# Spectral convolution on Trainium2: folded blocks of x, shifted copies from SBUF to SBUF, and 64x32 tiles in the last inverse step

## The chip, the cores and the metric

The kernel runs on one core of one Trainium2 chip. The core has a matrix engine (TensorE: PE for the matmuls, PEld for the weight loads), a vector engine (DVE), a scalar engine (ACT), a general engine (GpSimd, here POOL) and SyncE (SP), which issues most of the DMAs. The engines run side by side, each through its own instructions in order, and wait for each other through semaphores. Matmuls write to PSUM; the other engines copy the results to SBUF ("evict" them). The metric is the device time of one execution in microseconds (us).

## The reference

The input is four images of 512x512 pixels with 16 channels, in float32. Two layers follow each other, each with a group norm and a residual. The first is a convolution over the whole image with a filter that is given as a quotient of polynomials; it is done in the frequency domain:

```
H = rfft2(irfft2(rfft2(b)/rfft2(a)), s=(1024, 1024));  H_full = h0 + H[0]
X = rfft2(gn(x), s=(1024, 1024))
Y = einsum('...hwi,ijhw->...hwj', X, H_full)
y = irfft2(Y)[..., :512, :512, :];  x = x + y
```

The second layer is a 3x3 convolution that is normalized by the norms of patch and kernel and passed through an arccos.

## The kernel before

The kernel has five stages. The first evaluates the filter (and takes the statistics of the group norm beside it). `forward_phase` (L617 to L699) transforms x along the image's width with matmuls, after normalization. `conv_phase` (L705 to L966) does all that belongs to one frequency of the width: transform along the height, product with the filter, and inverse along the height. A further stage does the inverse along the width, and the last one the second layer. Only the second and third stage are spoken of below.

`forward_phase` goes over 16 blocks (4 images, 4 blocks of 128 lines). A block is loaded with four DMAs and folded about the middle of the width (additions on DVE, L652; subtractions on POOL, L654), transposed on PE (L661), and multiplied by the transform's matrix (L683). Products are evicted in turn by DVE (L691) and ACT (L693) and stored.

`conv_phase` works through 513 rows, one per frequency of the width (that of 0 in two parts). Of one row:
- `load_x` and `load_g` fetch x and the filter's line. `turn_x` (L773, L775) multiplies the small transform `dfs` by a phase that belongs to the row.
- `x_part` (L786) is the transform over 64 positions along the height into 128 frequencies f, with 4 matmuls into two PSUM tiles `px`; the evictions write slot 0 of `xe`, a tile of 128 partitions with 8 slots of 128x8 values.
- The other slots hold copies of slot 0 that are shifted by 16 partitions per slot. What would be shifted beyond the end comes from a late copy `xl` with another phase: `x_late` forms it on POOL with four products (L807) into a tile `xu`, one product over all (L808) and an addition (L809). Slot 4 is written by ACT, half from slot 0 and half from `xl` (`half_shift`, L818). The other six go through DRAM: POOL stores slot 0 and `xl` (L800), and SP loads them again, shifted, a row later (`load_xe`, L824).
- `g_part` (L838) transforms the filter's line in four groups, into a ring of three PSUM tiles `pg`, evicted into `gh`.
- `mix` (L854) is the product over channels: for each frequency one matmul with `gh` as weights, in four column quarters of 32. Four groups of 64 instructions; each is evicted into `yf`.
- `over_q` (L875 to L893) transposes `yf` into `pz`, and ACT (`zq`, L882), DVE (L883 to L887) and, at the end of the row, POOL (L891, L893) form sums and differences `z` and `zd`.
- `over_g` (L912) is the last inverse step with 8 matmuls of 128x64, into one PSUM tile `py`; the eviction goes into `yo`, and POOL stores it (L923).

`px`, `pz` and `py` share one ring of three PSUM tiles (`h_psf`, tag "full"). `evict` (L736, L738) gives two of three evictions to ACT and the third to DVE. `step(n)` interleaves five rows: `mix` of row n with `g_part` of n+1, `over_q` of n-1, `x_part`, `x_late` and `half_shift` of n+2, `turn_x` of n+3 and `over_g` of n-2, in four quarters k. The order on each engine isn't exactly that of the source; it is put in order when the program is built.

Of the kernel before, what the change touches and what calls it, by code (L numbers as in the profile page):

```python
# [48 lines left out]
B = 4  # L49
# [20 lines left out]
def constants():  # L70
# [80 lines left out]
    f, sb = np.arange(F), np.arange(S)  # L151
    d = np.zeros((2, S, F, 2))
    co, si = turn(np.outer(sb + 31.5, f), F)
    d[0, :, :, 0], d[0, :, :, 1] = co, -si
    d[1, :, :, 0], d[1, :, :, 1] = si, co
    c["dfs"] = np.stack([d, np.stack([d[..., 1], -d[..., 0]], -1)], 2).reshape(P, -1)
# [5 lines left out]
    ig = np.zeros((32, 2, 2, 4, 2, 2, 2, 16))  # L162
    for s0 in range(4):
        for cx in range(2):
            for c2 in range(2):
                n = gg[:, None] * s0 + 4 * gg[:, None] * s1[None, :] + 32 * (cx + c2)
                co, si = turn(n, F)
                for b2 in range(2):
                    ig[:, cx, b2, s0, c2, 0, b2, :] = co / F
                    ig[:, cx, b2, s0, c2, 1, b2, :] = si / F  # L170
# [446 lines left out]
def forward_phase(tc, cst, x, mvs, x_d):  # L617
    nc = tc.nc
    with ExitStack() as ctx:
        cp = ctx.enter_context(tc.tile_pool(name="x_const", bufs=1))  # L620
        xp = ctx.enter_context(tc.tile_pool(name="x_in", bufs=8))
        sm = ctx.enter_context(tc.tile_pool(name="x_small", bufs=B))
        up = ctx.enter_context(tc.tile_pool(name="x_u", bufs=4))
        tp = ctx.enter_context(tc.tile_pool(name="x_t", bufs=2))
# [12 lines left out]

        for b in range(B):
            scale, bias = norm[b]
            twice = sm.tile([P, 8], F32, name="twice")  # L640
            nc.vector.tensor_add(twice, bias, bias)
            for ht in range(4):
                xt = []
                for w in range(4):
                    t = xp.tile([P, P, C], F32, name="xt")
                    nc.sync.dma_start(out=t, in_=x[b, ht * P : (ht + 1) * P, w * P : (w + 1) * P, :])
                    xt.append(t)

                su = []
                for w in range(2):  # L650
                    u = up.tile([P, P, C], F32, name="xu")
                    nc.vector.tensor_add(u, xt[w], xt[3 - w][:, ::-1, :])  # L652
                    su.append(u)
                    nc.gpsimd.tensor_sub(xt[w], xt[w], xt[3 - w][:, ::-1, :])  # L654
                halves = su + xt[:2]
                xw = tp.tile([P, 4, C, P], F32, name="xw")
                for i4 in range(4):
                    for w in range(4):
                        pt = ps_x.tile([P, 4, P], F32, name="pt")
                        for i in range(4):  # L660
                            nc.tensor.transpose(pt[:, i], halves[w][:, :, 4 * i4 + i], ident)  # L661
                        for i2 in range(2):
                            g = 2 * i4 + i2
                            dst = xw[:, w, 2 * g : 2 * g + 2, :]
                            src = pt[:, 2 * i2 : 2 * i2 + 2, :]
                            if i2 == 0 and w < 2:
                                nc.scalar.activation(dst, src, AF.Identity,
                                                     scale=scale[:, g : g + 1], bias=twice[:, g : g + 1])
                            elif i2 == 0:
                                nc.scalar.activation(dst, src, AF.Identity, scale=scale[:, g : g + 1])  # L670
                            elif w < 2:
                                nc.vector.tensor_scalar(dst, src, scale[:, g : g + 1],
                                                        twice[:, g : g + 1], ALU.mult, ALU.add)
                            else:
                                nc.vector.tensor_scalar(dst, src, scale[:, g : g + 1], None, ALU.mult)
                for rc in range(4):
                    o = op.tile([P, 2, 16, 8, C], F32, name="xo")
                    for c in range(2):
                        col = (2 * rc + c) * P
                        for i4 in range(4):  # L680
                            pf = ps_f.tile([P, 4, 16, 8], F32, name="pf")
                            for w in range(2):
                                nc.tensor.matmul(  # L683
                                    pf.rearrange("p i s t -> p (i s t)"), fwd[:, w, col : col + P],
                                    xw[:, 2 * c + w, 4 * i4 : 4 * i4 + 4, :].rearrange("p i h -> p (i h)"),
                                    start=(w == 0), stop=(w == 1),
                                )
                            dst = o[:, c, :, :, 4 * i4 : 4 * i4 + 4]
                            src = pf.rearrange("p i s t -> p s t i")[:, :, ::-1, :]
                            if c == 0:  # L690
                                nc.vector.tensor_copy(dst, src)  # L691
                            else:
                                nc.scalar.copy(dst, src)  # L693
                    for c in range(2):
                        nc.sync.dma_start(
                            out=dram(x_d[rc], None, c * X_ROW // 2 + (16 * ht * B + b) * C * 8,
                                     [B * C * 8, 16], [1, C * 8]),
                            in_=o[:, c].rearrange("p s t i -> p s (t i)"),
                        )  # L699
# [5 lines left out]
def conv_phase(tc, cst, g_d, x_d, y_d):  # L705
    nc = tc.nc
    with ExitStack() as ctx:
# [11 lines left out]
        dfs = load_const(nc, cp, cst, "dfs").rearrange("p (v n) -> p v n", v=2)  # L719
        dg = load_const(nc, cp, cst, "dg")  # L720
        ident = load_const(nc, cp, cst, "ident")
        ig = load_const(nc, cp, cst, "ig").rearrange("p (s c n) -> p s c n", s=4, c=2)
        late = load_const(nc, cp, cst, "late").rearrange("p (v f) -> p v f", v=3)

        xf_d = [tc.dram_tile([16 * C, XF], F32, name=f"xf_d{n}") for n in range(4)]
# [26 lines left out]
        def load_x(n):  # L752
# [3 lines left out]
            if plane is None:  # L756
                nc.sync.dma_start(out=t, in_=dram(x_d[rc], r, 0, [w, P], [1, w]))
            else:
                nc.gpsimd.memset(t[S:], 0.0)
                nc.sync.dma_start(out=t[:S], in_=dram(x_d[rc], r, plane * S * w, [w, S], [1, w]))  # L760
            state["x", n] = x

        def turn_x(n):
# [8 lines left out]
            t = xlp.tile([P, 2 * F], F32, name="turn")  # L772
            nc.scalar.activation(t, dfs[:, 1], AF.Identity, scale=own[:, 1, at])  # L773
            m = xlp.tile([P, 2 * F], F32, name="dfs_n", bufs=2)
            nc.vector.scalar_tensor_tensor(m, dfs[:, 0], own[:, 0, at], t, ALU.mult, ALU.add)  # L775
            state["dfs", n] = m

        def x_part(n, b):

            if b == 0:  # L780

                state["xe", n] = xep.tile([P, 8, F, 2, 2, 2], F32, name="xe")
            if b % 2 == 0:
                state["px"] = ps_f.tile([P, 2, F, 2], F32, name="px", tag="full")
# [661 lines left out]
```

## Time and profile before

| what | us |
|---|---|
| median of three runs (lowest, highest) | 18,372.5 (18,348.46, 18,387.49) |
| the profiled execution | 18,378.82 |
| its span | 18,377.0 |
| filter and statistics, 0 to 5,320 | 5,320 |
| forward, 5,320 to 6,415 | 1,095 |
| conv, 6,415 to 15,535 | 9,120 |
| inverse along the width, 15,535 to 16,610 | 1,075 |
| second layer, 16,610 to 18,377 | 1,767 |

Over the whole span PE is busy 88%, PEld 63%, DVE 61%, ACT 52% and POOL 57%. A busy share is an average over stages, so the conv stage is looked at by itself, and within it single rows. In the profile "PEclk" is the clock that PE was granted (1.00 is full speed), and "idle before, releaser" is the time in which an instruction's engine stood still ahead of it, with the instruction whose end released it.

### The profile page before, as it was taken

The numbers are of one execution on the slowest core, as the hardware profiler recorded it, in microseconds if no ns is written. First come the engines' busy times: TensorE is split into PE (matmuls) and PEld (weight loads), VectorE is DVE, ScalarE is ACT, GpSimd is POOL, SyncE is SP. The second block draws the span as 40 slices with busy tenths as digits, with TensorE's granted clock in tenths as the row PEclk, the third lists the DMA queues.
The fourth block names the chain that finished last, engine by engine and source line by source line (L and its number), as shares of the span: only waits on it lengthen the run. The fifth ranks groups of instructions, "written<-read, shape, count | busy, mean of one in ns | idle before, by whom it ended". The sixth has DMA issues, their size and how long they took to land. (4 is left out here: it accounts for less than half of the span.)

```text
span 18377.0 us, 546088 instructions
## 1 busy us (share of the span) xinstructions
PE 16100.0 (88%) x233100; PEld 11615.5 (63%) x233100; DVE 11247.9 (61%) x23131; ACT 9599.6 (52%) x19919; POOL 10502.4 (57%) x10653
## 2 busy tenths in 40 slices
PE   7788888888889988888888888888888988988888
PEld 4444444444444467777777777777767776877777
DVE  8877777777833355555555555555555554246887
ACT  4556555555632255555555555555555554106788
POOL 5566666666621166666666666666666664026776
PEclk6888988888999999999999999999999999998999
DMA  4655555555676588888888888888888887795431
GB/s 123 201 162 165 162 165 162 164 163 161 167 221 184 167 319 320 318 321 324 316 321 318 319 325 323 325 325 323 323 323 314 325 320 289 257 324 192 160 129 69
DMA packets 2918877, 4543.47 MB, mean 247 GB/s; under 512 B 117634, under 2 KB 2086492, under 8 KB 2809694
## 3 DMA queue, kind: packets, MB, share of 16 engines
q1 hardware_dynamic: 2686254, 3768.39, 60.7%
q0 software_dynamic: 174896, 605.89, 8.7%
q10 hardware_dynamic: 55296, 134.24, 2.2%
q8 instruction: 1835, 30.06, 0.6%
q14 instruction: 596, 4.88, 0.1%
HBM read 3030.71 MB, written 1477.31 MB: 245 GB/s over the span
## 5 line engine op out<-in xcount | busy, mean ns | idle before, releaser
L838 PE MATMUL pg<-c_dg,g 64*128 64x128 f32 x32832 | 2836.9, 291 | 326.6 <-ACT gh L738 163.0
L854 PE MATMUL pm<-xe,gh 128*32 128x64 f32 x131328 | 2397.8, 222 | 587.8 <-issue 354.6
L854 PEld LDWEIGHTS pm<-xe,gh 128*32 128x32 f32 x131328 | 2011.9, 110 | 1165.3 <-issue 972.6
L838 PEld LDWEIGHTS pg<-c_dg,g 64*128 64x128 f32 x32832 | 2283.3, 190 | 670.4 <-issue 253.4
L456 PE MATMUL pt<-ev_in,c_todd 128*128 128x512 f32 x4096 | 2191.1, 681 | 350.4 <-ACT ot L461 323.9
L883 DVE TENSOR_TENSOR z<-zq,pz 128x256 f32<-128x256 f32 x2052 | 861.4, 420 | 2608.4 <-ACT zq L882 2531.1
L736 DVE COPY gh<-pg 128x512 f32<-128x512 f32 x2046 | 1410.1, 689 | 1312.1 <-PE pg L838 1308.2
L379 POOL TENSOR_TENSOR x<-ab,ab 128x512 f32<-128x512 f32 x1024 | 1561.1, 1524 | 1081.7 <-ACT ab L362 1029.0
L807 POOL TENSOR_TENSOR xu<-xe,c_late 128x256 f32<-128x256 f32 x2052 | 1389.5, 702 | 860.2 <-ACT xe L738 834.6
L377 DVE RECIPROCAL dn<-dn 128x256 f32<-128x256 f32 x1024 | 1781.8, 1740 | 0.0
L456 PEld LDWEIGHTS pt<-ev_in,c_todd 128*128 128x128 f32 x4096 | 792.4, 210 | 1483.1 <-issue 640.1
L738 ACT COPY yf<-pm 128x512 f32<-128x512 f32 x2046 | 1210.9, 592 | 924.0 <-PE pm L854 909.2
L362 ACT COPY ab<-pab 128x512 f32<-128x512 f32 x2048 | 1127.9, 617 | 858.7 <-PE pab L353 609.1
L818 ACT COPY xe<-xl 64x1024 f32<-64x1024 f32 x513 | 538.5, 1050 | 1872.5 <-POOL xl L809 1872.5
L738 ACT COPY gh<-pg 128x512 f32<-128x512 f32 x2058 | 1200.0, 583 | 398.4 <-PE pg L838 389.5
L875 PE MATMUL pz<-c_ident,yf 128*128 128x128 f32 x8208 | 1377.4, 291 | 30.3 <-issue 28.5
L404 PE MATMUL pg<-c_dinv,sp 64*128 64x128 f32 x16384 | 1192.7, 301 | 117.8 <-ACT sp L393 117.8
L404 PEld LDWEIGHTS pg<-c_dinv,sp 64*128 64x128 f32 x16384 | 1084.7, 209 | 313.2 <-PE pab L353 134.1
L376 DVE TENSOR_TENSOR m<-ab,ab 128x512 f32<-128x512 f32 x1024 | 1271.4, 1242 | 0.0
L809 POOL TENSOR_TENSOR xl<-xl,xu 128x1024 f32<-128x1024 f32 x513 | 1208.9, 2357 | 40.2
L383 POOL TENSOR_TENSOR m<-m 128x256 f32<-128x256 f32 x1024 | 747.0, 730 | 746.4 <-DVE m L376 746.2
L1289 PE MATMUL pc<-l_band,xn 128*128 128x160 f32 (+2 forms) x6144 | 1072.9, 333 | 53.7 <-DVE e_o L1344 53.5
(204 smaller groups left out, 31381.8 us busy)
## 6 DMA issues: line engine op xcount, KB each, us to landing
xe<-xf_d SPq DMA_DIRECT2D x1026, 1536.0 KB, 8.4
g<-g_d SPq DMA_DIRECT2D x511, 1024.0 KB, 9.8
g_d<-st SPq DMA_DIRECT2D x64, 4096.0 KB, 31.3
ev_in<-g_d SPq DMA_DIRECT2D x1024, 256.0 KB, 4.6
g_d<-ot SPq DMA_DIRECT2D x1024, 256.0 KB, 2.5
xf_d<-xe POOLq DMA_DIRECT2D x513, 448.0 KB, 8.3
xf_d<-xl POOLq DMA_DIRECT2D x513, 448.0 KB, 5.2
x_d<-xo SPq DMA_DIRECT2D x128, 1024.0 KB, 5.1
```

The source lines that it names most:

```text
L376: nc.vector.tensor_mul(w["m"], b, a)
L377: nc.vector.reciprocal(w["dn"], w["dn"])
L379: nc.gpsimd.tensor_mul(w["x"], b, a[:, :, ::-1])
L404: nc.tensor.matmul(pg[u][:, n, k].rearrange("p a x -> p (a x)"), w["sp"][q, k, c, :], dinv[q, 2 * kp + k, c, :], start=(c == 0), stop=(c = ...
L456: nc.tensor.matmul(pt, todd[:, c, kc, hh * P : hh * P + P], ev[:, kc, c], start=(kc == 0), stop=(kc == 1),)
L736: nc.vector.tensor_copy(dst, src)
L738: nc.scalar.copy(dst, src)
L807: nc.gpsimd.tensor_mul(u[:, :, h, c], xe[:, :, h, 1 - c], bc(late[:, 1 + c], 2, [P, F, 2]))
L809: nc.gpsimd.tensor_add(xl.rearrange("p f h c k -> p (f h c k)"), xl.rearrange("p f h c k -> p (f h c k)"), u.rearrange("p f h c k -> p (f ...
L838: nc.tensor.matmul(pg[c][:, j % 4], g[half, j], dg[half], start=True, stop=True)
L854: nc.tensor.matmul(pm[32 * q : 32 * q + 32, g % 8], gh[:, f].rearrange("p c j -> p (c j)"), xe[:, :, f].rearrange("p t h c k -> p t (h c k ...
L875: nc.tensor.transpose(pz[:, t % 4].rearrange("p v q x -> p (v q x)"), y[:, at].rearrange("p g x -> p (g x)"), ident)
```

## The change

In the forward stage the blocks of 128 lines are folded about the middle of the image: block ht and block 3-ht are transformed together, ACT copies the product of the one, and DVE adds and subtracts that of the other, mirrored. So the two halves that are stored are the even and the odd part along the height.

In the conv stage `x_part` then transforms 32 positions for each parity, with 64 rows of contraction and one PSUM tile per part (real, imaginary). The phase that belongs to the row moves from the input's transform to the output's: `turn_ig` replaces `turn_x`. `over_g` works in tiles of 64x32 into two PSUM tiles. The shifted copies no longer go through DRAM: `shift` copies from slot 0 and `xl` to the other slots within SBUF, with twelve DMAs that SP issues. The intermediate product `u` has no tile of its own but is written into slot 4 of `xe`, and `xl` has two buffers. `x_part` stands ahead of `over_q` in the step. The inverse stage and the constants follow the new layout of y.

```diff
--- before
+++ after
-        xp = ctx.enter_context(tc.tile_pool(name="x_in", bufs=8))
+        xp = ctx.enter_context(tc.tile_pool(name="x_in", bufs=6))
-        up = ctx.enter_context(tc.tile_pool(name="x_u", bufs=4))
-        tp = ctx.enter_context(tc.tile_pool(name="x_t", bufs=2))
+        up = ctx.enter_context(tc.tile_pool(name="x_u", bufs=3))
+        tp = ctx.enter_context(tc.tile_pool(name="x_t", bufs=5))
+        ap = ctx.enter_context(tc.tile_pool(name="x_a", bufs=4))
...
+        def folded(b, ht):
+
...
+            return su, xt[:2]
+
+        def turned(halves, scale, bias):
+
+            xw = tp.tile([P, 2, C, P], F32, name="xw")
...
+            return xw
+
+        def transform(xw, c, rc, i4):
...
+            return pf.rearrange("p i s t -> p s t i")[:, :, ::-1, :]
+
         for b in range(B):
-            for ht in range(4):
...
+            for ht in range(2):
+                near, far = folded(b, ht), folded(b, 3 - ht)
+                for c in range(2):
+                    both = [turned(h[c], scale, (twice, None)[c]) for h in (near, far)]
+                    for rc in range(4):
+
+                        sums = [op.tile([P, 16, 8, C], F32, name=f"xo{k}") for k in range(2)]
                         for i4 in range(4):
...
+                            pa, pb = (transform(xw, c, rc, i4) for xw in both)
+                            pb = pb[:, ::-1]
+                            a = ap.tile([P, 16, 8, 4], F32, name="xa")
+                            nc.scalar.copy(a, pa)
+                            i = slice(4 * i4, 4 * i4 + 4)
+                            nc.vector.tensor_add(sums[0][:, :, :, i], a, pb)
+                            nc.vector.tensor_sub(sums[1][:, :, :, i], a, pb)
+                        for k in range(2):
+                            part = ((0, 3), (2, 1))[c][k]
+                            nc.sync.dma_start(
+                                out=dram(x_d[rc], None, part * X_ROW // 4 + (16 * ht * B + b) * C * 8,
+                                         [B * C * 8, 16], [1, C * 8]),
+                                in_=sums[k].rearrange("p s t i -> p s (t i)"),
+                            )
...
-        xf_d = [tc.dram_tile([16 * C, XF], F32, name=f"xf_d{n}") for n in range(4)]
...
-        def turn_x(n):
+        def turn_ig(n):
...
             own, at = state["own", n // 64], slice(n % 64, n % 64 + 1)
-            t = xlp.tile([P, 2 * F], F32, name="turn")
-            nc.scalar.activation(t, dfs[:, 1], AF.Identity, scale=own[:, 1, at])
-            m = xlp.tile([P, 2 * F], F32, name="dfs_n", bufs=2)
-            nc.vector.scalar_tensor_tensor(m, dfs[:, 0], own[:, 0, at], t, ALU.mult, ALU.add)
-            state["dfs", n] = m
-
-        def x_part(n, b):
-
...
+            t = xlp.tile([P, 256], F32, name="turn")
+            nc.scalar.activation(t, ig[:, 1], AF.Identity, scale=own[:, 1, at])
+            m = xlp.tile([P, 4, 2, 32], F32, name="ig_n", bufs=2)
+            nc.vector.scalar_tensor_tensor(m.rearrange("p s c n -> p (s c n)"), ig[:, 0], own[:, 0, at], t,
+                                           ALU.mult, ALU.add)
+            state["ig", n] = m
+
+        def x_part(n):
+
+            state["xe", n] = xep.tile([P, 8, F, B, 2], F32, name="xe")
+            px = [ps_f.tile([P, B, F], F32, name=f"px{c}", tag="full") for c in range(2)]
+            for b in range(B):
+                for c in range(2):
+                    half = slice(64 * c, 64 * c + 64)
+                    nc.tensor.matmul(px[c][:, b], state["x", n][half, b], dfs[half], start=True, stop=True)
+            for c in range(2):
+                evict(state["xe", n][:, 0, :, :, c], px[c].rearrange("p b f -> p f b"))
+            del state["x", n]
 
         def x_late(n):
 
             xe = state["xe", n][:, 0]
...
+            fl = xe.rearrange("p f b c -> p f (b c)")
+
+            xl = xlp.tile([P, F, B, 2], F32, name="xl", bufs=2)
+            u = state["xe", n][:, 4]
             for c in range(2):
...
+                nc.gpsimd.tensor_mul(u[:, :, :, c], xe[:, :, :, 1 - c], bc(late[:, 1 + c], 2, [P, F, B]))
+            nc.gpsimd.tensor_mul(xl.rearrange("p f b c -> p f (b c)"), fl, bc(late[:, 0], 2, [P, F, 2 * B]))
+            nc.gpsimd.tensor_add(xl.rearrange("p f b c -> p (f b c)"),
+                                 xl.rearrange("p f b c -> p (f b c)"),
+                                 u.rearrange("p f b c -> p (f b c)"))
             state["xl"] = xl
 
         def half_shift(n, half):
 
             dst, src = ((slice(0, 64), state["xe", n][64:, 0]), (slice(64, P), state["xl"][:64]))[half]
-            nc.scalar.copy(state["xe", n][dst, 4].rearrange("p f h c k -> p (f h c k)"),
-                           src.rearrange("p f h c k -> p (f h c k)"))
-
-        def load_xe(n):
-            src = xf_d[n % 4]
-            for t in (1, 5):
-                nc.sync.dma_start(
-                    out=state["xe", n][:, t : t + 3].rearrange("p t f h c k -> p t (f h c k)"),
-                    in_=bass.AP(tensor=src.tensor, offset=src.offset + t * C * XF,
-                                ap=[[XF, P], [C * XF, 3], [1, XF]]),
-                )
+            nc.scalar.copy(state["xe", n][dst, 4].rearrange("p f b c -> p (f b c)"),
+                           src.rearrange("p f b c -> p (f b c)"))
+
+        def shift(n, half):
+
+            xe, src = state["xe", n], state["xl"] if half else state["xe", n][:, 0]
+            for t in (1, 2, 3, 5, 6, 7):
+                at = C * t
+                to, of = ((slice(0, P - at), slice(at, P)), (slice(P - at, P), slice(0, at)))[half]
+                nc.sync.dma_start(out=xe[to, t].rearrange("p f b c -> p (f b c)"),
+                                  in_=src[of].rearrange("p f b c -> p (f b c)"))
 
         def g_part(n, j):
 
...
             if g % 8 == 7:
-                evict(state["y", n][:, :, g - 7 : g + 1].rearrange("p t g x -> p g t x"),
-                      pm.rearrange("p g t (h x) -> p g (t h) x", h=2))
+                evict(state["y", n][:, :, g - 7 : g + 1].rearrange("p m g c -> p g m c"), pm)
...
             if k == 0:
-                state["py"] = ps_f.tile([P, 2, 2, 8, C], F32, name="py", tag="full")
-            z, d, py = state["z", n], state["zd", n], state["py"]
-            odd, c2 = k // 2, k % 2
-            for half in range(2):
-                s0 = 2 * half + odd
...
+                state["py"] = [ps_f.tile([P, 2, 8, C], F32, name=f"py{h}", tag="full") for h in range(2)]
+            z, d, m = state["z", n], state["zd", n], state["ig", n]
+            c2 = k
+            for s0 in range(4):
+                at = (s0 + 1) % 4
+                if at % 2 == 0:
+                    zs = z[:, :, at + c2]
...
-                nc.tensor.matmul(
-                    py[64 * half : 64 * half + 64, odd], ig[:, s0, c2],
-                    zs.rearrange("p (t h) j -> p h t j", h=2),
-                    start=(c2 == 0), stop=(c2 == 1),
-                )
-            if k < 3:
+                for half in range(2):
+                    q = slice(64 * half, 64 * half + 64)
+                    nc.tensor.matmul(
+                        state["py"][half][32 * s0 : 32 * s0 + 32], m[q, s0, c2],
+                        zs[q].rearrange("p (t h) j -> p h t j", h=2), start=(c2 == 0), stop=(c2 == 1),
+                    )
+            if k == 0:
                 return
...
+            del state["z", n], state["zd", n], state["ig", n]
+            yo = yop.tile([P, 2, 2 * P], F32, name="yo")
+            for half in range(2):
+                evict(yo[:, half].rearrange("p (h j t) -> p h j t", h=2, j=C),
+                      state["py"][half].rearrange("p h t j -> p h j t"))
+            w = 2 * P
             if plane is None:
-                nc.gpsimd.dma_start(out=dram(y_d[rc], r, 0, [4 * P, P], [1, 4 * P]), in_=yo)
+                nc.gpsimd.dma_start(out=dram(y_d[rc], r, 0, [w, P], [P * w, 2], [1, w]), in_=yo)
...
-            if row(1):
-                load_xe(n + 1)
...
                 if row(1):
                     for j in range(4):
                         g_part(n + 1, 4 * k + j)
+                if row(2) and k == 0:
+                    x_part(n + 2)
                 if row(-1):
                     for t in range(4):
                         over_q(n - 1, 4 * k + t)
                 if row(2) and k == 0:
-                    for m in range(B):
-                        x_part(n + 2, m)
+                    shift(n + 2, 0)
                     x_late(n + 2)
+                    shift(n + 2, 1)
                 if row(2) and k >= 2:
                     half_shift(n + 2, k - 2)
-                if row(3) and k == 2:
-                    turn_x(n + 3)
+                if row(-1) and k == 2:
+                    turn_ig(n - 1)
                 if row(-2) and k == 2:
-                    for m in range(4):
+                    for m in range(2):
                         over_g(n - 2, m)
```

More of the change, by code (lines that the diff above doesn't have):

```diff
@@ L161, in constants @@
     gg, s1 = np.arange(32), np.arange(16)
-    ig = np.zeros((32, 2, 2, 4, 2, 2, 2, 16))
+    ig = np.zeros((2, 32, 2, 2, 4, 2, 2, 16))
     for s0 in range(4):
@@ new lines, in transform @@
+        def transform(xw, c, rc, i4):
+            col = (2 * rc + c) * P
+            pf = ps_f.tile([P, 4, 16, 8], F32, name="pf")
+            for w in range(2):
+                nc.tensor.matmul(
+                    pf.rearrange("p i s t -> p (i s t)"), fwd[:, w, col : col + P],
+                    xw[:, w, 4 * i4 : 4 * i4 + 4, :].rearrange("p i h -> p (i h)"),
+                    start=(w == 0), stop=(w == 1),
+                )
+            return pf.rearrange("p i s t -> p s t i")[:, :, ::-1, :]
```

175 lines of the change are left out of this document (60 added, 115 removed).

## Prediction

> **What bounds the kernel now.** Three views were read in this order: the table by stretches, the list of waits inside the conv stretch, and the timeline of one row by engine. Columns of the first: stretch, length, busy time of PE, PEld, DVE, ACT and POOL (instructions), granted PE clock, DMA share, GB/s.
>
> ```profile
> 5320.00:6415.00 1095.00, 1032.81 (x3074) 515.48 (x3074) 402.38 (x551) 279.71 (x513) 152.58 (x36) 0.97 0.60 182
> 6415.00:15535.00 9120.00, 8121.43 (x184680) 6487.67 (x184680) 4934.76 (x13342) 4784.71 (x8721) 5777.09 (x5653) 0.98 0.86 320
> 12009.83:12026.92 17.09, 15.71 (x361) 12.51 (x361) 9.79 (x27) 9.24 (x17) 11.27 (x11) 1.00 0.89 335
> ```
>
> The first line is the forward stretch, the second the conv stretch, the third one of its rows. Conv takes 9,120 us for 513 rows, 17.78 us each; a quiet row takes 17.09 with PE at work for 15.71. No engine is full, so a loop through several engines sets the pace. The waits of the conv stretch (waiter and line, releaser and line: total us, how often, longest) name its members:
>
> ```profile
> DVE z L883 <- ACT zq L882: 2531.1, 1579, 6.7
> ACT xe L818 <- POOL xl L809: 1872.5, 513, 6.5
> POOL xu L807 <- ACT xe L738: 834.6, 507, 7.1
> PE pm L854 <- DMA xe<-xf_d: 96.4, 70, 3.2
> ```
>
> ACT stands still 3.65 us in every row for POOL's last addition; a DMA holds PE in 70 cases for 96 us in all. The transfers that the change removes are hidden already. The timeline of that row, POOL, then ACT, then PE (start, busy time, instructions, idle before and releaser):
>
> ```profile
> 12014.17 1.36 POOL L807 TENSOR_TENSOR xu<-xe,c_late 128x256 f32<-128x256 f32 x2 [1.40 <-ACT xe L738]
> 12015.65 0.57 POOL L800 DMA_DIRECT2D xf_d<-xe  x1
> 12016.25 1.35 POOL L807 TENSOR_TENSOR xu<-xe,c_late 128x256 f32<-128x256 f32 x2
> 12017.54 1.98 POOL L808 TENSOR_TENSOR xl<-xe,c_late 128x1024 f32<-128x1024 f32 x1
> 12019.60 2.36 POOL L809 TENSOR_TENSOR xl<-xl,xu 128x1024 f32<-128x1024 f32 x1
> ```
>
> ```profile
> 12021.99 1.05 ACT L818 COPY xe<-xl 64x1024 f32<-64x1024 f32 x1 [3.73 <-POOL xl L809]
> 12023.07 0.58 ACT L738 COPY yf<-pm 128x512 f32<-128x512 f32 x1
> 12023.55 0.59 ACT L738 COPY gh<-pg 128x512 f32<-128x512 f32 x1
> 12024.02 0.39 ACT L882 COPY zq<-pz 128x256 f32<-128x256 f32 x1
> ```
>
> ```profile
> 12024.19 1.16 PE L838 MATMUL pg<-c_dg,g 64*128 64x128 f32 x14 [0.33 <-ACT gh L738]
> 12026.92 0.77 PE L854 MATMUL pm<-xe,gh 128*32 128x64 f32 x40 [0.57 <-ACT zq L882]
> ```
>
> Read as a loop: POOL starts the late copy at 12014.17 and ends the addition at 12021.96, 7.79 us. ACT then makes the shift it had waited for and works off what stood behind it, so the next row's mix starts at 12026.92, 4.96 us after the addition. Mix, g_part, transposes, x_part and the eviction lead to POOL's next start at 12031.26, 4.34 us later. 7.79 + 4.96 + 4.34 = 17.09, the length of the row.
>
> **The change, part by part.**
>
> *Forward.* The transform's matmul instructions (2,048; the page has two for each matmul, and so do all counts below) and the DMAs stay the same in number. Evictions of the products go from 256 copies on DVE and 256 on ACT to 256 copies on ACT and 512 additions or subtractions on DVE. At 0.69 us each (the DVE eviction of 128x512) DVE goes from 402 to some 580 us, beside PE's 1,033. The smaller buffer pools (6 input blocks, 3 folded) make the fold of the next pair wait for the transposes. Bounds: 0, if PE still covers it, to +107 us, eight pairs whose four additions on DVE (3.32 us each) all lie bare. I take +40, not far from the middle, as nothing in the trace places it.
>
> *Conv, removed in every row.* From POOL two DMA issues (0.57 and 0.58) and four multiplications of 0.70; from the queues 0.9 MB of stores and 3.1 MB of loads, hidden; from PE sixteen py instructions of 128x64 (1.96 us in the row) and eight px of 256 columns (1.89); turn_x, whose place an equal turn_ig takes.
>
> *Conv, added in every row.* On PE sixteen x_part instructions in g_part's form (16 take 1.16) and thirty-two of py in 64x32 tiles: by the mix (64 in 1.10) at least 0.55, by the old py at most 1.96; I take 1.0, near the mix, since four quarters work beside each other in both. PE's work falls from 15.7 to 15.7 - 1.96 - 1.89 + 1.16 + 1.0 = 14.0 us. On POOL two multiplications of 128x512 for the four of half that size: 1.27 (the sum L893) to 1.52 each (L379), against 4 x 0.70 = 2.80; I take 1.35, so the late copy takes 2.7 + 1.98 + 2.36 = 7.0 us with the gaps (bounds 6.8 and 7.4). On SP twelve SBUF copies for two loads: 3.0 MB in 64 to 448 KB. The trace has no such copy; by the old xe load (3 MB inside 8.4 us with others beside it) they take about 8 us of the engines. Lower bound 4 us, half of that; upper bound 16, twice. The whole DMA load falls from 0.86 x 17.78 = 15.3 to some 12.5 us per row and stays covered by a row's slack, for a shift of row n+2 is first read by a mix one row later.
>
> *The wait that is moved.* The multiplied copy u no longer has a tile of its own; it is written into slot 4 of xe, the slot that half_shift(n, 0) then overwrites. So half_shift(0) has to wait for POOL's addition, where before only half_shift(1) did. On ACT's queue half_shift(0) stands ahead of the second block's gh eviction and its zq (in the built program it carries the wait on POOL). In the row above those, gh at 12017.41 and zq at 12017.88, were done before ACT's wait began. Now gh(1) and zq(1) wait for the addition too. Who waits for these: PE's g_part of the third block (a pg buffer), and, since px and py now take eight tiles a row in a ring of three instead of seven, py, whose second tile takes over pz(1)'s place: it needs zq(1) and the DVE chain behind it.
>
> From the end of the addition: half_shift 1.05, gh 0.58, zq 0.38, DVE's five operations 0.42 + 0.29 + 0.29 + 0.30 + 0.28 = 1.58, together 3.6; then py 1.0, the last mix 1.1, its g_part 1.16, the eviction 0.6: 7.5 us to the next row's mix. In the row kinds where both half_shifts stand ahead it is up to 1.5 more (1.05 for the second, 0.5 for a second gh on ACT). The built order repeats six kinds of row, half of them of either sort; the mean is 8.3. Before it was 4.96.
>
> From that mix to POOL's start: mix 1.1, g_part 1.16, x_part 1.16, eviction 0.6, 4.0; in some kinds x_part stands ahead of g_part. I take 3.9 (before 4.34).
>
> Sum: 7.0 + 8.3 + 3.9 = 19.2 us at full clock, against 17.09. PE works 14.0 of it, so it stands idle 5.2 us, in one stretch while POOL ends its addition.
>
> *The clock.* What such a stretch costs, the trace of before shows (first line a gap, second line what follows; same columns as above):
>
> ```profile
> 9000.00:9001.60 1.60, 0.04 (x1) 0.03 (x1) 1.44 (x5) 0.36 (x1) 0.70 (x1) 1.00 0.78 310
> 9001.90:9005.30 3.40, 3.40 (x74) 3.00 (x62) 0.43 (x2) 0.58 (x1) 1.54 (x2) 0.50 0.53 164
> ```
>
> The granted clock changes in steps of 3.41 us. All 91 drops to 0.50 in the conv stretch followed a step in which PE was busy 0.57 or less; it came back after a step busy 0.92 or more. An idle stretch of 5.2 us always leaves one step under 0.3, so every row drops. At half clock the mix takes 1.7 to 1.9 us for 1.10 and g_part 1.9 to 2.1 for 1.16. The half clock falls on py, the last mix and g_part, all in the loop: 3.3 us of matmuls that grow by 0.5 (clock back at once) to 2.5 us (half clock throughout). I take 2.1, since the drop lasts at least one whole step.
>
> The Trainium skill, "TensorE: Matmul & The Clock Gate", Part 1, says that after one idle window of about 3.4 us PE's clock is halved. Read as a rule for wholly idle windows it would spare the rows whose 5.2 us straddle two windows and bring the drop in (5.2 - 3.41)/3.41, about half, of the rows and make the sum 20.3 instead of 21.3 us a row; the stretch at 9001.90, after only 1.56 us of idleness, speaks against that reading.
>
> Row: 19.2 + 2.1 = 21.3 us; 513 of them 10,930, which is 1,810 more than 9,120. With 40 for the forward stretch, 18,379 (the profiled execution, 6 us or 0.03% above the median of 18,372.5) becomes 20,230.
>
> The inverse reads the same bytes in the same number of loads: 0.
>
> The Trainium skill, "DMA: Bandwidth & Descriptors", Bandwidth, asks for transfers of 1 MiB or more for 75% of the peak, which all twelve copies miss. By it they would cost more than 3.0 MB at three quarters of its 435 GB/s, an estimate of 9.2 us a row; no run here shows it, and the forecast's 8 us would not decide anything at that price either.
>
> **The rivals.**
>
> *The clock holds* (0.25). If buffers spread the idleness, or the idle stretch ends in two, no row drops: 19.2 us, 513 x 19.2 = 9,850, with 40 forward 19,150. For it: PE has two pm and three pg buffers to work ahead in. Against it: those are full after one block.
>
> *The moved wait is harmless and the kernel is faster* (0.12). If py and g_part find free buffers, the addition is followed by before's 4.96 us: 7.0 + 4.96 + 3.9 = 15.9, 513 x 15.9 = 8,157, and the whole 17,460 (16,900 if the row comes down to 14.8, PE's 14.0 with some stalls; 17,900 if it stays at 16.8). It decides once the stretch from addition to mix is below 17.78 - 7.0 - 3.9 = 6.9 us. For it: PE's work falls by 1.7 us a row and POOL's by 1.2. Against it: the ring and the queue order, counted above.
>
> *The SBUF copies set the pace* (0.10). If they take 16 to 18 us of the engines for 8, the DMA load becomes 20.5 to 22.5 us, and at the share of 0.89 that the row above reached, 23 to 25 us a row: 21,100 to 22,100. For it: every copy moves single rows of 4 KB, to and from one memory. Against it: the old load moved the same rows within 8.4 us.
>
> **How the numbers follow.** The forecast has 0.50; its own range is 19,700 to 20,800 (row from 20.3 to 22.4). The rivals have 0.25, 0.12 and 0.10, the rest 0.03. From 18,700 to 21,400 the first two cases lie inside with the lower end of the third; outside are the faster case and about half of the slow copies, 0.18 with the rest. About 0.2% (37 us) is what a measurement can tell from no change; that close to 18,372 lies only a stretch of 6.8 to 7.0 us, 0.02. Faster 0.12, slower 0.86.
>
> **What would show it.** In the changed profile: half_shift waits for the addition (L813) some 5.6 us a row, 2,900 us in all, against 1,872; PE's clock in the conv stretch falls to about 0.88; PE is busy under 80% of it; the conv stretch takes 10,930 us, the forward one 1,135. py at 1.0 us, the multiplications at 1.35 and the copies at 8 us a row can be read off. The prediction is wrong if ACT's wait leaves gh(1) and zq(1) behind it without PE standing still, if the clock stays at 0.98, or if PE waits for the copies.

## The result, and the profile after

The changed kernel takes 20,233 us (median of four runs, 20,219 to 20,254) against 18,360 for the kernel before on the same chip: 1.1022 times as long, 95% interval 1.1000 to 1.1045. The forecast was 20,230. The number was right and the mechanism behind it was there; but the experiments show a second mechanism, which the prediction had put down as hidden, that alone would have made the kernel nearly as slow. That this one lay beneath the first, and left the number nearly as it was, is luck.

The stretches of the changed kernel (forward, then conv, from its first x_part to its last mix as before; columns as in the prediction):

```profile
5320.00:6445.00 1125.00, 1037.82 (x3068) 518.88 (x3068) 535.20 (x799) 276.42 (x511) 152.28 (x38) 0.97 0.58 173
6445.00:17375.00 10930.00, 8261.22 (x196992) 6494.31 (x196992) 4902.42 (x13515) 4851.46 (x9063) 5013.59 (x3605) 0.86 0.90 224
```

Nearly all of the loss lies in the conv stretch: 10,930 us for 9,120. PE does hardly more work by its busy time, at a clock of 0.86 for 0.98. And the DMA share went up, from 0.86 to 0.90, in a longer stretch and with fewer bytes (224 GB/s for 320). The waits of that stretch:

```profile
DVE z L885 <- ACT zq L884: 4087.7, 1906, 7.1
ACT xe L821 <- POOL xl L813: 2518.0, 513, 6.1
PE pg L841 <- ACT gh L748: 896.6, 253, 9.5
PE py L916 <- ACT yf L748: 630.0, 165, 5.3
PE py L916 <- DVE z L889: 362.7, 94, 5.6
PE pm L857 <- issue: 398.4, 344, 4.4
```

ACT now waits 4.9 us a row at half_shift(0), and behind it PE waits for the evictions of g_part or for py's PSUM tile, as the ring and the queue had said. The timeline of one row, POOL, ACT, then PE (the lines that matter here; PE's py between 12026.55 and 12028.23 is left out):

```profile
12013.64 2.23 POOL L811 TENSOR_TENSOR xe<-xe,c_late 128x512 f32<-128x512 f32 x2
12017.89 2.34 POOL L813 TENSOR_TENSOR xl<-xl,xe 128x1024 f32<-128x1024 f32 x1
```

```profile
12020.26 1.04 ACT L821 COPY xe<-xe 64x1024 f32<-64x1024 f32 x1 [5.07 <-POOL xl L813]
12021.21 0.58 ACT L748 COPY yf<-pm 128x512 f32<-128x512 f32 x1
12021.80 1.04 ACT L821 COPY xe<-xl 64x1024 f32<-64x1024 f32 x1
12022.86 0.59 ACT L748 COPY gh<-pg 128x512 f32<-128x512 f32 x1
```

```profile
12023.50 2.07 PE L841 MATMUL pg<-c_dg,g 64*128 64x128 f32 x14 [4.94 <-ACT gh L748]
12025.51 1.11 PE L877 MATMUL pz<-c_ident,yf 128*128 128x128 f32 x4
12028.23 1.10 PE L857 MATMUL pm<-xe,gh 128*32 128x64 f32 x64
```

From POOL's first multiplication to the end of its addition 6.6 us; ACT makes two shifts and two evictions; PE comes back after 4.94 us of idleness, at half clock (14 of g_part's 16 instructions in 2.07, where all 16 take 1.16 at full clock), and only the mix at 12028.23 runs at full clock. Between 12023.50 and 12028.23 PE did 4.73 us of work without a break that at full clock takes 1.02 (the 14) + 0.66 (the transposes) + 1.1 (py) = 2.8.

Averaged from the trace over rows 10 to 500 (first mix to POOL's first multiplication, from there to the end of the addition, from there to the next row's first mix), with the share of the time at half clock, the mean 4 KB packet of the hardware queue and the busy time of the 16 DMA engines per row:

| | mix to POOL | POOL | addition to mix | row, us | half clock | packet | DMA per row |
|---|---|---|---|---|---|---|---|
| before | 4.48 | 7.81 | 5.42 | 17.70 | 0.04 | 176 ns | 15.3 us |
| forecast | 3.9 | 7.0 | 8.3 + 2.1 | 21.3 | | | 12.5 us |
| changed | 4.11 | 6.57 | 10.55 | 21.23 | 0.27 | 294 ns | 19.1 us |

The last column doesn't fit the prediction at all. So the question for the chip: what of the loss comes from the moved wait (theory W), and what from the copies, which load the DMA engines by 19.1 us of a row of 21.2 (theory D)?

### The profile page after: what moved, and what is told of

It is laid out like the page before. It is cut to its first block, busy times and chain, and to the rows that moved or that the text cites. A ratio compares the mean times of both kernels' runs of the same rounds, so it can differ in the third digit from the quotient of the medians.

```text
span 20229.1 us, 580754 instructions
## 1 busy us (share of the span) xinstructions
PE 16258.3 (80%) x245412; PEld 11633.5 (58%) x245412; DVE 11350.9 (56%) x23558; ACT 9667.5 (48%) x20261; POOL 9741.2 (48%) x8607
## 5 line engine op out<-in xcount | busy, mean ns | idle before, releaser
L857 PE MATMUL pm<-xe,gh 128*32 128x64 f32 x131328 | 2709.3, 236 | 582.7 <-issue 398.4
L857 PEld LDWEIGHTS pm<-xe,gh 128*32 128x32 f32 x131328 | 2270.2, 120 | 1341.3 <-issue 1024.0
L929 POOL DMA_DIRECT2D y_d<-yo x511 | 382.4, 748 | 4004.3 <-ACT yo L748 3598.7
L748 ACT COPY gh<-pg 128x512 f32<-128x512 f32 x2736 | 1536.3, 587 | 1329.3 <-PE pg L841 1312.4
L916 PE MATMUL py<-zd,ig_n 64*32 64x256 f32 x4104 | 1107.3, 564 | 996.6 <-ACT yf L748 630.0
L821 ACT COPY xe<-xe 64x1024 f32<-64x1024 f32 x513 | 535.1, 1043 | 2518.0 <-POOL xl L813 2518.0
L746 DVE COPY gh<-pg 128x512 f32<-128x512 f32 x1368 | 942.2, 689 | 1277.3 <-PE pg L841 1275.0
L811 POOL TENSOR_TENSOR xe<-xe,c_late 128x512 f32<-128x512 f32 x1026 | 1134.1, 1127 | 428.0 <-ACT xe L748 326.7
L893 POOL TENSOR_TENSOR zd<-z 128x512 f32<-128x512 f32 x513 | 648.0, 1263 | 1383.7 <-DVE z L885 1383.5
L813 POOL TENSOR_TENSOR xl<-xl,xe 128x1024 f32<-128x1024 f32 x513 | 1206.1, 2351 | 40.1
```

Of the source, the lines that this page charges most:

```text
L811: nc.gpsimd.tensor_mul(u[:, :, :, c], xe[:, :, :, 1 - c], bc(late[:, 1 + c], 2, [P, F, B]))
L813: nc.gpsimd.tensor_add(xl.rearrange("p f b c -> p (f b c)"), xl.rearrange("p f b c -> p (f b c)"), u.rearrange("p f b c -> p (f b c)"))
L857: nc.tensor.matmul(pm[32 * q : 32 * q + 32, g % 8].rearrange("p m c -> p (m c)"), gh[:, f].rearrange("p c j -> p (c j)"), xe[:, :, f].rear ...
```

## The experiments

Ratios are to the kernel before, in runs on the same chip; the medians of before were 18,404 us in the first four runs, 18,384 in the next four and 18,308 to 18,313 in the last ones.

**The wait taken away, the copies left.** First by a tile of its own for u, of half the size and used twice:

```diff
-            u = state["xe", n][:, 4]
+            nc.gpsimd.tensor_mul(xl.rearrange("p f b c -> p f (b c)"), fl, bc(late[:, 0], 2, [P, F, 2 * B]))
             for c in range(2):
...
+                u = xlp.tile([P, F, B], F32, name="xu")
+                nc.gpsimd.tensor_mul(u, xe[:, :, :, 1 - c], bc(late[:, 1 + c], 2, [P, F, B]))
+                nc.gpsimd.tensor_add(xl[:, :, :, c], xl[:, :, :, c], u)
```

> The changed kernel, but the multiplied copy u has a tile of its own (half the size, used twice, one addition for each part), so half_shift(0) no longer waits for POOL; only half_shift(1) does. Theory W (the moved wait on ACT's queue sets the row): g_part's second block is evicted before the wait, but half_shift(1) still stands ahead of zq(1) in most rows, so only part comes back: about 0.5 to 1.5 us a row, 19,450 to 19,950 us in all, and half_shift(0)'s wait for POOL is gone from the list. Theory D (the copies from SBUF to SBUF fill the DMA engines, 0.90 busy in the conv stretch or 19.2 us of a row, and set the pace): no more than 0.5% from the changed kernel's 20,233, as the copies stay.

It took 20,075 us, 1.0919 (1.0900 to 1.0939): a tenth of the loss came back, less than W's range has and more than D's, so it doesn't decide. half_shift(0) no longer waits for POOL, but half_shift(1) still does, 4.1 us a row, ahead of zq(1) in four of the six kinds of row; the wait was only put off. Then with both shifts on POOL:

```diff
-            nc.scalar.copy(state["xe", n][dst, 4].rearrange("p f b c -> p (f b c)"),
+            nc.gpsimd.tensor_copy(state["xe", n][dst, 4].rearrange("p f b c -> p (f b c)"),
                            src.rearrange("p f b c -> p (f b c)"))
```

> The changed kernel with both half_shifts done by POOL, behind its addition, instead of ACT. ACT waits for POOL nowhere ahead of gh(1) and zq(1); the twelve copies stay. Theory W: the row falls to what PE's 14 us and some stalls make, 15 to 17 us, so the conv stretch to 7,700 to 8,700 and the kernel to 17,000 to 18,050. Theory D: the copies need their 19.2 us of engine time in every row, and at a busy share of 0.94 to 0.98 the row stays at 19.6 to 20.4 us: 19,360 to 19,770.

19,877 us, 1.0806 (1.0789 to 1.0822). ACT's wait for POOL is gone and the row still takes 20.5 us, just above theory D's range and far from the 15 to 17 of W. Its conv stretch, with the columns of the first table:

```profile
6487.00:17003.00 10516.00, 7959.27 (x196816) 6425.07 (x196816) 4965.23 (x13483) 3898.65 (x8022) 6056.36 (x4607) 0.89 0.98 232
```

The DMA engines are full, at 0.98. What PE waits for in this stretch, first the longest of its waits, then the one for a copy:

```profile
PE pm L857 <- issue: 1662.3, 778, 8.5
PE pm L857 <- DMA xe<-xl: 6.0, 4, 1.8
```

**The copies taken away.** Stores and loads through DRAM as before the change, u and xl in tiles of their own, the folding and the new matmul forms kept; then also both shifts on POOL.

```diff
+            if row(1):
+                load_xe(n + 1)
...
-                    shift(n + 2, 0)
                     x_late(n + 2)
-                    shift(n + 2, 1)
```

> The changed kernel with the shifted copies through DRAM again (stores by POOL, two loads by SP, u and xl in tiles of their own, as before the change); folding, x_part, turn_ig and py in 64x32 tiles stay. half_shift(0) doesn't wait for POOL, half_shift(1) does, behind zq(1). Theory W: POOL's late copy 7.1 us, then the 4.96 us of before to the mix, then 3.9: 16.0 us a row, conv 8,200 and the kernel about 17,500 (17,200 to 17,900). Theory D gives the same to within 200 us, since the copies are gone. If neither the wait nor the copies but the folding, x_part or py costs the time, it stays above 19,500.

> As the run with copies through DRAM, and both half_shifts done by POOL. ACT waits for POOL nowhere. POOL's work in a row rises to some 14 us. Theory W: PE's 14 us or POOL's bound the row at 15 to 16 us, 17,000 to 17,550. Theory D: the same, the load on the DMA engines is that of before, 15.3 us a row. If POOL's extra copies are slower than 1.6 us each, it is slower than the run without them.

They took 18,709 us (1.0171) and 18,678 us (1.0146, 1.0130 to 1.0162). The copies are worth 1.0806 - 1.0146, 6.6 points, where there is no wait. But both runs are far above the 17,500 that was expected, and slower than before: without wait and without copies the folding, x_part and py gain nothing. The row is 18.2 us, and PE's busy time has fallen as hoped. The conv stretch of the run with both edits, same columns:

```profile
6500.00:15826.00 9326.00, 7616.03 (x196712) 6178.03 (x196716) 5024.39 (x13474) 3927.44 (x8012) 6664.21 (x5623) 0.93 0.85 312
```

PE's timeline in it shows the kind of its gaps:

```profile
12008.55 0.42 PE L864 MATMUL pm<-xe,gh 128*32 128x64 f32 x15
12010.93 0.89 PE L864 MATMUL pm<-xe,gh 128*32 128x64 f32 x49 [1.95 <-issue]
```

PE stops in the middle of a mix, where the profile shows nothing that it waits for. Of the 1,685 us of PE's gaps over 0.3 us in this conv stretch, 1,482 us ended between 1.15 and 1.6 us after the end of a 16 KB packet of the instruction queue; for a moment taken at random the chance of that is 0.07. It points to PE waiting for its own code, which comes through the same DMA engines. In the run with the shifts on POOL it was 1,731 of 2,492 us, and a wait for a copy is hardly on the list: full DMA engines seem to reach PE by way of its code. In the kernel before it was 627 of 943, in the changed one 594 of 2,550.

> The run with DRAM copies and half_shifts on POOL, with the filter's line loaded for every second row only (the other rows use the line of the row before, so the result is that of another filter); the load on the DMA engines falls from 15.4 to some 12.8 us a row. In the run without this, 1,480 of the 1,685 us of PE's gaps over 0.3 us in the conv stretch ended 1.15 to 1.6 us after the end of a 16 KB packet of the instruction queue. Theory F (PE waits for its own code, fetched through the same DMA engines behind the data): these stalls shrink by more than half, the kernel falls to 17,500 to 18,100. If PE's gaps come from something else (semaphores, PSUM), it stays within 150 us of 18,680.

18,312 us, 0.9954. 1.9 points came back, some 350 us, which is neither case: the gaps behind a code packet fell from 1,482 to 1,371 us only; the rest are other gaps (from about 200 to 70 us) and a clock of 0.95 for 0.93. That lighter DMA load helps is shown; that it does so through the code alone is not.

**The wait alone.** u in slot 4 of xe on top of the DRAM copies, and the stores issued by SP, which puts half_shift(0) ahead of gh(1) and zq(1) in every row, as in the changed kernel:

```diff
-                nc.gpsimd.dma_start(out=xf_d[n % 4][half * P :, :][at], in_=t[at].rearrange("p f x -> p (f x)"))
+                nc.sync.dma_start(out=xf_d[n % 4][half * P :, :][at], in_=t[at].rearrange("p f x -> p (f x)"))
...
-            u = xlp.tile([P, F, B, 2], F32, name="xu")
+            u = state["xe", n][:, 4]
```

> The run with copies through DRAM, but u again in slot 4 of xe, so that half_shift(0) waits for POOL's addition, and the stores issued by SP, with which ACT's queue has half_shift(0) ahead of gh(1) and zq(1) in every row, as in the changed kernel. The wait without the copies from SBUF. Theory W, as predicted: 19.2 us of chain and about 2 us of lost clock a row, so 1.09 to 1.10 of the kernel before, 20,050 to 20,300 us. Theory D (the copies cost the time, the wait lies mostly in their shade): no more than 400 us above the 18,709 of the run without the wait, at most 1.04.

19,973 us, 1.0869 (1.0847 to 1.0890), slightly under theory W's range and far from D's. The conv stretch, and in it the moved wait and PE's stops of the kind above:

```profile
6505.00:17143.00 10638.00, 8257.05 (x196698) 6540.66 (x196702) 4915.96 (x13473) 4843.22 (x9035) 5003.30 (x3580) 0.89 0.74 274
```

```profile
ACT xe L828 <- POOL xl L819: 2392.4, 506, 5.9
PE pm L864 <- issue: 849.0, 633, 3.8
```

The DMA engines are at 0.74, packets take 180 ns, and the row is 20.8 us: 4.5 + 6.6 + 9.7, near the loop of the prediction. So the wait alone costs 7.2 points over the run with neither (which has its shifts on POOL and its stores issued there), the copies alone 6.6, both together 8.8: each covers most of the other.

ACT's order isn't quite that of the changed kernel, though. Here half_shift(1) always stands behind gh(1) and zq(1). In the changed kernel it does so in 238 of the rows 10 to 499; in the other 252 both shifts stand ahead of zq(1). From the addition to the next row's mix the first sort takes 9.8 us there, and 9.7 here; the second takes 11.3. So among rows of the same sort the copies add nothing to this stretch, and the run with the wait alone is somewhat too cheap. On the other side 1,197 of its 2,360 us of PE's gaps end behind a code packet, twice as much as in the changed kernel. The 7.2 points are therefore the price of the wait only roughly.

> The changed kernel with the filter's line loaded for every second row only (the others use the line of the row before, so the result is that of another filter). The load on the DMA engines falls by some 2.5 us a row. If the wait of half_shift(0) alone sets the row and the copies lie beside it, less than 100 us come back: 20,130 to 20,250. If the copies hold the rows back as well, it comes near the run that had the wait without the copies, 1.087 of the kernel before: 19,900 to 20,050.

1.0881 (1.0865 to 1.0897): the second case, 1.4 points less than the changed kernel. So the DMA load still costs something on top of the wait. How much of that is due to the copies isn't shown. The rows of this run alternate between 17.0 and 24.3 us; their mean of 20.6 lies near the 20.8 of the wait alone, but it need not be the same loop.

**The kernel before, with one edit each.** u into slot 4, or both shifts on POOL.

> The kernel before, with u written into slot 4 of xe, nothing else: half_shift(0) waits for POOL's addition, both half_shifts then stand one behind the other, but behind zq(1) and ahead of the third block's evictions. Theory W: the wait itself stays where it was, and one half_shift of 1.05 us is added between the addition and what follows: 0.5 to 1.05 us a row, 18,600 to 18,950. If a wait on ACT's queue costs PE nothing while PE waits for code or DMA anyway: within 100 us of the kernel before.

1.0384 (1.0363 to 1.0405), 19,075 us: more than expected, 1.34 us a row for a shift of 1.05; the share at half clock went from 0.04 to 0.10, which fits the rest.

> The kernel before, with both half_shifts done by POOL behind its addition; ACT waits for POOL nowhere. If POOL, ACT and PE form the loop that was read off the row of 17.09 us, it opens, and PE's 15.7 us a row with some gaps set the pace: 16.2 to 16.8 us, 17,600 to 17,900. Theory F: PE's code sets a floor near the present rows, since 627 of its 943 us of gaps over 0.3 us in the conv stretch already end behind a code packet; 18,050 to 18,300.

1.0025 (1.0015 to 1.0035): neither case; opening the loop gained nothing. The row stays at 17.76 us, where the quiet row of 17.09 had been taken for a loop through ACT. With ACT's wait gone other limits stand at the same height. 672 of 999 us of PE's gaps end behind a code packet, and PE's waits for the shifted loads, 96 us in 70 cases before, became:

```profile
PE pm L854 <- DMA xe<-xf_d: 379.6, 210, 4.7
```

**What makes the copies slow.** The DRAM loads cut as the copies are, into twelve with 16 to 112 partitions; then into six with all 128:

```diff
-            for t in (1, 5):
+            for half in range(2):
+                for t in (1, 2, 3, 5, 6, 7):
+                    at = C * t
+                    to, of = ((slice(0, P - at), at), (slice(P - at, P), P))[half]
...
```

> The run with DRAM copies and half_shifts on POOL, with the two loads of a row cut into the twelve of the changed kernel (same partitions, same 64 to 448 KB, issued by SP), but read from DRAM. Tells what makes the copies slow: in the changed kernel a 4 KB packet from SBUF to SBUF took 294 ns, against 176 to 179 ns for the same number of packets from DRAM. Small, uneven transfers as the cause: packets near 290 ns, the DMA share near 0.97 and the kernel near 19,870 us, as with the copies from SBUF. SBUF at both ends as the cause: packets near 180 ns, the kernel within 250 us of 18,680, with 4 us more of issuing on SP.

> As the run with the twelve loads from DRAM, but each slot of xe in one load over all 128 partitions, 512 KB: six loads a row, even ones, in place of two of 1536 KB. With twelve uneven loads a 4 KB packet took 275 ns, with two it took 177 ns. If the uneven ranges of partitions make the packets slow, they take about 180 ns here and the kernel is within 200 us of the run with two loads, 1.0146 of the kernel before (18,500 to 18,800). If the number or size of the transfers does it, they lie between, near 220 to 260 ns, and the kernel at 19,200 to 20,200.

Twelve took 1.1291 (1.1274 to 1.1308), slower than the changed kernel, with packets of 275 ns; six took 1.0244 with packets of 179 ns. The main hardware queue on the two pages (packets, MB, share), first twelve, then six:

```profile
q1 hardware_dynamic: 2768366, 3768.52, 67.6%
```

```profile
q1 hardware_dynamic: 2719118, 3768.33, 60.3%
```

The same megabytes, with a larger share of a longer span (20,657 us for 18,737). So it isn't that both ends lie in SBUF, nor that a transfer has 512 KB for 1,536: the slow packets come with the cut into twelve. That cut changes three things at once, the ranges of partitions, their number (12 for 6) and the smallest size (64 KB for 512), and no run takes them apart. A range short of 128 isn't slow by itself: the stores of 112 partitions to DRAM are most of the 4 KB packets of POOL's queue, which took 176 ns in the run with the twelve loads. How the ranges are spread over the engines the trace doesn't tell.

**The clock.** Three matmuls of 128x512 into the idle stretch of the run with the wait alone:

```diff
+            for i in range({8: 2, 16: 1}.get(g, 0)):
+                nc.tensor.matmul(pm.rearrange("p g m c -> p (g m c)"), ident,
+                                 gh[:, :16].rearrange("p f c j -> p (f c j)"), start=True, stop=True)
```

> The run dram_wait with three extra matmuls of 128x512 per row on PE, two ahead of the second block's mix and one ahead of the third's, into the tile that the mix overwrites; each takes about 1.2 us, 3.6 us of a row, and falls mostly into the time in which PE stands still. Tells the price of the clock. If the halved clock behind the idle stretch costs some 2 us a row, as predicted, the granted clock rises from 0.89 to 0.95 or more and the kernel gets faster in spite of the added work, by 300 to 900 us: 19,050 to 19,650. If the clock costs nothing on the path, the kernel is the same or slower, 19,950 to 20,700.

20,540 us, 1.1215 (1.1196 to 1.1234), with a clock of 0.897 for 0.895. The filler ran ahead of the idle stretch and didn't shorten it (PE's gaps of over 2 us are 2.9 us long in the mean, for 2.8 without the filler), so the condition of the test didn't come about; it doesn't settle the price of the clock. What stands for that is the timeline above, 4.73 us for 2.8 on the path behind an idle stretch, and PE's busy time: the run with the wait alone and the run with neither have the same matmuls, to within 14 instructions, and PE is busy 8,257 us in the one and 7,616 in the other, at half clock for 0.22 and 0.14 of the time. These 641 us are half of the 1,312 us between their conv stretches; how much of them lies on the path isn't shown.

## Why the prediction was right, and where it was wrong

*The loop.* Held, term by term: POOL 6.57 for 7.0 (the multiplications took 1.13 us each, under the lower bound of 1.27 that came from other POOL operations), addition to mix 10.55 for 10.4, mix to POOL 4.11 for 3.9, the row 21.23 for 21.3. The two sorts of rows are there as well, about half of each, 1.5 us apart (9.8 and 11.3) as forecast. The run with the wait alone shows that the loop makes a row of about this length without the copies from SBUF. In the row shown PE came back 3.3 us after the addition. The sum has 3.6 there, but for the way by zq and DVE; here the way was ACT's alone, two shifts and two evictions (1.04 + 0.58 + 1.04 + 0.59).

*The clock.* 0.86 for 0.88; 27% of the time at half clock, 5.7 us a row, and 1.9 us lost on the path in the row shown, for 2.1. PE stood idle 5.2 us a row as forecast, but not in one stretch: the longest of a row had 3.8 us in the mean. Even so 478 of the 490 rows have a step at half clock. The first rival, that the clock holds, fell. The Trainium skill's "TensorE: Matmul & The Clock Gate", Part 1, read as a gate on wholly idle windows, would have made rows of 20.3; the row of 21.23 and the 27% agree with a drop in nearly every row. Only 116 of the 548 drops in the changed conv stretch followed a step in which PE did nothing; half of them followed steps in which it was busy 0.22 or more, up to 0.64. The measurement decides. (In the kernel before there are 95 drops in the stretch, not 91, all after steps busy 0.10 to 0.57.)

*The forward stretch.* From its first transform matmul to the first x_part 1,130 us for 1,087: 43 for 40. DVE has 535 us for the 580 forecast.

*The DMA load: wrong.* "About 8 us of the engines" for the copies and "stays covered" failed. 768 packets at 294 ns on 16 engines are 14.1 us, and the load rose from 15.3 to 19.1 us a row instead of falling to 12.5. The upper bound of 16 held, but the rival with slow copies had 0.10 and was taken for a case of its own, in which they alone set the pace; the runs show two limits of nearly one height. That the forecast hit the number all the same is due to that: the larger of the two decides, and the smaller lies mostly beneath it. Luck has a part in it: at the forecast's own upper bound of 16 us the load would have been some 21 us a row (an estimate: 19.1 + 16 - 14.1), all of the loop's row.

*The faster rival: wrong in its price.* With the wait made harmless it gave 17,460. The run with the shifts on POOL, which has no such wait on ACT, took 19,877, with 9.2 us from addition to mix. Without copies that stretch fell to 5.8 us, under the 6.9 of the rival's condition, and still 18,678 remained. It had left out the DMA engines and what seems to be PE's code, and the run that opened the loop in the kernel before shows that taking a wait out of a loop brings only what the next limit allows, there nothing.

*The reading of before.* The loop of 17.09 us was read off a row that it describes, but it wasn't the only limit there, as the kernel before with both shifts on POOL shows.

The Trainium skill, "DMA: Bandwidth & Descriptors", Bandwidth, asks for transfers of 1 MiB or more for 75% of the peak. The estimate from it, more than 9.2 us for the copies, was too low like the forecast's 8; and the six loads of 512 KB, half of that size, had packets as fast as those of 1,536 KB. The size that the rule goes by doesn't tell the slow packets from the fast ones here.

## What to carry to other kernels

Price a removed wait against the next limit, not against zero, and count a new transfer in engine time from packets of transfers cut the same way: twelve loads of 16 to 112 partitions cost 1.6 times the engine time of two whole ones with the same bytes. When a buffer is shared to save space, look at what stands behind the new wait on the waiting engine's queue: here two evictions, a ring of PSUM tiles and PE's clock. A prediction can hit its number with one of two limits of equal height unseen; only runs that take each away alone tell, and in such a run the order on the waiting engine's queue has to be that of the kernel in question.

## What the runs showed of the hardware

A 4 KB packet took 174 to 182 ns in loads of all 128 partitions (512 or 1,536 KB) and 275 to 305 ns where a row's transfers were cut into twelve of 16 to 112 partitions, from DRAM and from SBUF alike. PE's stops that the profile calls "issue" end, for the most part, 1.15 to 1.6 us after a 16 KB packet of the instruction queue; such a packet took 994 ns in the run with DRAM copies and 1,260 ns where the DMA engines were 0.98 busy. PE ran 32 py instructions in 64x32 tiles in 1.1 us at full clock, against 1.95 us for the 16 of 128x64. Its clock changed in steps of 3.41 us, and it dropped after steps in which PE did nothing as well as after steps in which it was busy up to 0.64.
